# An attention block with its feed-forward and a second attention: VectorE's part of the softmax shift one round later, and sums pinned behind the last minimum of scores

## The chip, the cores and the metric

The kernel runs on one core of a Trainium2 chip. The core has a matrix engine (TensorE, PE in the profile; its weight loads are PEld), a vector engine (VectorE, DVE), an engine for activation functions (ScalarE, ACT), a general engine (GpSimd, POOL) and an engine that here only issues transfers (SyncE, SP). Each engine takes its instructions in the order in which they stand in its own queue and waits, at an instruction, for the semaphores that this one names; all that stands behind it on this engine waits too. The metric is the device time of one execution in microseconds (us), lower is better.

## The reference

The reference works on x of shape (2, 1024, 1024), all in float32:

```python
x = x + attn_a(layernorm(x))   # 32 heads of 32, rotary, causal, plus an adapter prefix of 10 tokens
x = x + ffn(layernorm(x))      # x @ W_base.T + b, plus 8 low-rank experts weighted by a sparsemax router
x = x + attn_b(layernorm(x))   # 8 heads of 16, not causal, softmax divided by sqrt(128)
x = x + ffn(layernorm(x))      # the same weights again
```

Only the attentions matter for the change. For each head they need softmax(q k^T * scale) v, with the row's maximum subtracted before the exponential.

## The kernel before, in words

**Stages.** Attention A with the projections of its queries, keys and values fills roughly the first 1320 us; then come its output projection, the first feed-forward, attention B and the second feed-forward, partly interleaved.

**Units and rounds.** Attention is cut into units. A unit of A is one batch element b, one group g of four heads (128 partitions) and one half n of the 1024 queries: 32 units, named A{b}_{g}_{n}. A unit of B is named in the same manner (8 units). Every unit passes over its scores twice. The first pass (`s_mm`, `s_post`) multiplies queries by keys into the PSUM tile `sc` (L308); VectorE writes the masked, scaled and negated scores to `pr` and keeps the running minimum in `part` or `nmax` (L321, one instruction for each score tile and head, with a short one that reads the accumulator); ScalarE takes the exponential and sums it into `sums` (L329). From `nmax` and the logarithm of `sums` the unit makes its shift (`shift`, L332 to L351): m = nmax + bias - ln(sums), split into three bfloat16 parts so that they add up to it. TensorE transposes the shift into rows (`shift_rows`, tile `st_A`; evacuated by L218 or L220). The second pass (`t_mm`) computes the scores transposed in the tile `st` with the shift added as a small matmul (L376 and L378), so that one exponential on ScalarE (L489) gives finished probabilities `pt`, which GpSimd masks on the diagonal (L385) and TensorE multiplies with the values (L400).

The loop of `attend` walks through rounds r. Each round has the scores of two heads of one step of the first pass and two heads of one step of the second. `sc` and `st` share a tag of two PSUM buffers and are drawn in turn, so the scores of round r+1 reuse the tile of the scores of round r, and TensorE's L308 waits there until VectorE's minima of round r are done. A unit with n=0 has fewer keys than one with n=1; after the last row of scores of a unit its shift is written in the same round.

**Fill.** Between rounds `Filler` lets TensorE work on the projections of later groups. These are Strassen-like: `seven` does seven block products instead of eight; its sums and combinations on VectorE are `factors` (sums of weight blocks, L594 and L597, tiles s, s_v, wqk, wv) and the lines L652 to L671, which combine PSUM results y and z with SBUF blocks. `rotate` (L792, L793 on VectorE; L796, L797 on GpSimd) applies the rotary embedding to queries and keys. Weights arrive by `v_load` (L682, a single buffer of 1 MB for two groups) and `qk_load` (L688, two buffers).

**The adapter.** `adapter_scores` multiplies queries by adapter keys into the tile `as`, and VectorE takes the maximum (L735), the difference (L737), the sum (L740) and the reciprocal (L741), with an exponential on ScalarE between (L738). `as`, the transposes of the shift and those of x for the second batch element share one PSUM bank.

**What sets the order.** The queues of TensorE and, in attention A, of GpSimd are written by hand, in program order. The queues of VectorE and ScalarE are ordered by a planner, which lists instructions by when it believes them to be ready. Two ways hold it to an order: `tc.keep_in_program_order(r)` puts r behind the instruction of its engine that was traced just before it, and `tc.add_manual_dep` puts one instruction behind a named one. Neither makes an instruction wait for the other to finish. Before, the sums and combinations used the first: each stands behind whatever VectorE instruction was traced before it, which at the end of a unit is the last of its shift.

## Time and profile before

| what | us |
|---|---|
| median of 3 runs | 2521.57 (2521.26 to 2530.68) |
| the profiled execution's own time | 2524.32 |
| its span, first to last instruction | 2522.6 |
| TensorE busy | 2444.0 |
| VectorE busy | 1334.8 |
| ScalarE busy | 1092.2 |
| GpSimd busy | 501.0 |
| TensorE busy between 100 and 1320 us (attention A) | 1179.0 of 1220 |
| VectorE's waits for the logarithm at L346, 29 times | 47.6 |
| VectorE's waits for the logarithm at L340 (attention B), 7 times | 14.2 |

The granted TensorE clock of the execution was 0.992 of full speed. In a row of the profile "L321 DVE ... out<-in" names the line of the kernel, the engine, what is written and what is read; a row of waits gives who waited for whom, the total, how often and the longest; in a row of the order of time come start, duration, instruction and, in brackets, the idle time of the engine before it with what ended it.

### The profile page before, as it was taken

To read this page: it belongs to the slowest core of one execution; us is meant where nothing else is said; L and a number is where in the kernel's file an instruction comes from. 1 tells how busy PE (TensorE), PEld (TensorE's weight loads), DVE (VectorE), ACT (ScalarE), POOL (GpSimd) and SP (SyncE) were. 2 spreads that over 40 slices of the span, in tenths; PEclk is the share of its full clock that TensorE was granted. 3 is DMA by queue.
4 is the path that set the end of the run, shared out by engine and by line. 5 is a ranking of instruction groups with operands and counts; after the bars stand their busy time and mean duration, and the time that the engine had idled before them with its cause. 6 is when DMAs were issued, how large, how long until landed. Compare 5 with 4: busy or idle time off the path is not lost.

```text
span 2522.6 us, 60430 instructions
## 1 busy us (share of the span) xinstructions
PE 2444.0 (97%) x25477; PEld 1107.0 (44%) x25477; DVE 1334.8 (53%) x4120; ACT 1092.2 (43%) x2085; POOL 501.0 (20%) x800
## 2 busy tenths in 40 slices
PE   7889999999999999999999999999999999999999
PEld 4424444455344444445433445575333553333344
DVE  7665665566655666565520013456555765654243
ACT  2346666565655666566642000012445535554200
POOL 1332322222323233222200002101000101111120
PEclk9999999999999999999999999999999999999999
DMA  6622323332423333333222551120000310212121
GB/s 211 205 89 77 97 84 92 94 90 90 138 85 107 90 98 89 94 89 111 86 72 75 172 185 51 58 92 35 34 34 35 127 43 26 93 43 84 43 101 42
DMA packets 142512, 224.34 MB, mean 89 GB/s; under 512 B 12832, under 2 KB 73376, under 8 KB 142240
## 3 DMA queue, kind: packets, MB, share of 16 engines
q1 hardware_dynamic: 142240, 220.48, 27.3%
q8 instruction: 199, 3.26, 0.5%
q14 instruction: 73, 0.60, 0.1%
HBM read 168.01 MB, written 52.43 MB: 87 GB/s over the span
## 4 chain that ended last, share of the span: by engine, by line
PE 84%; DVE 7%; ACT 5%; DMA 2%; issue 1%; POOL 1%; SPq 0%; DVEq 0%; ACTq 0%; POOLq 0%
PE fo_f L207 11%; PE st L378 9%; PE fo_f L209 8%; PE sc L308 7%; PE op L207 6%; PE y_A L400 5%; PE y L209 5%; PE z L209 3%; PE op L209 3%; PE st L376 3%; PE x L209 3%; ACT pr_A L329 2%; PE y_B L400 2%; PE bq L207 2%; PE y_v L209 2%; DVE pr_A L321 2%
## 5 line engine op out<-in xcount | busy, mean ns | idle before, releaser
L489 ACT ACTIVATE pt<-st 128x1024 f32<-128x1024 f32 (+1 forms) x418 | 426.3, 1020 | 663.6 <-PE st L378 497.7
L329 ACT ACTIVATE pr_A<-pr_A,nmax_A 128x896 f32<-128x896 f32 (+7 forms) x512 | 390.0, 765 | 68.4 <-DVE nmax_A L321 67.7
L308 PE MATMUL sc<-kT,qT 32*128 32x512 f32 (+3 forms) x1536 | 329.3, 525 | 18.5 <-DVE nmax_A L321 13.6
L321 DVE CUSTOM_DVE_ANT_0 pr_A<-sc,mask 128x512 f32<-128x512 f32 (+3 forms) x512 | 250.9, 536 | 180.5 <-PE sc L308 94.4
L378 PE MATMUL st<-qT,kT 32*128 32x512 f32 (+3 forms) x1536 | 310.1, 491 | 0.0
L207 PE MATMUL fo_f<-wb,xt_f 128*128 128x512 f32 x558 | 252.9, 596 | 0.4 <-ACT hwT_f L1135 0.4
L321 DVE CUSTOM_DVE_ANT_0 pr_A<-sc,mask,part_A 128x512 f32<-128x512 f32 (+1 forms) x256 | 156.3, 647 | 162.4 <-PE sc L308 114.8
L225 POOL TENSOR_TENSOR xf<-xf,b_base 128x256 f32<-128x256 f32 x128 | 89.3, 729 | 762.0 <-DVE xn_f L247 457.8
L209 PE MATMUL fo_f<-wb,xt_f 128*32 128x512 f32 x1864 | 223.1, 598 | 0.0
L385 POOL TENSOR_SCALAR_AFFINE_SELECT pt<-pt 128x256 f32<-128x256 f32 x256 | 100.3, 410 | 543.7 <-ACT pt L489 543.7
L329 ACT ACTIVATE pr_B<-pr_B,nmax_B 128x1024 f32<-128x1024 f32 x128 | 145.5, 1140 | 39.9 <-DVE nmax_B L321 39.8
L400 PE MATMUL y_A<-pt,v 128*32 128x512 f32 (+3 forms) x1536 | 160.0, 502 | 1.3 <-POOL pt L385 1.3
L207 PEld LDWEIGHTS fo_f<-wb,xt_f 128*128 128x128 f32 x558 | 103.5, 193 | 113.7 <-issue 113.1
L308 PE MATMUL sc<-kq,qk 32*128 32x512 f32 x512 | 145.1, 643 | 3.5 <-DVE nmax_B L321 3.2
L207 PE MATMUL op<-wp,yt 128*128 128x512 f32 x338 | 145.7, 592 | 0.0
L378 PE MATMUL st<-rows_B,kq 32*128 32x512 f32 x512 | 144.7, 641 | 0.2 <-ACT pt L489 0.2
L378 PEld LDWEIGHTS st<-qT,kT 32*128 32x128 f32 x1536 | 133.9, 186 | 16.7 <-issue 11.6
L239 ACT ACTIVATE lv_f<-ve_f 128x1 f32<-128x1 f32 x32 | 6.5, 203 | 309.1 <-DVE ve_f L237 309.1
L376 PE MATMUL st<-rows_A,ones 3*128 3x512 bf16 (+3 forms) x768 | 128.0, 330 | 10.8 <-DVE nmax_A L321 10.8
L321 DVE CUSTOM_DVE_ANT_0 pr_B<-sc,mask,part_B 128x512 f32<-128x512 f32 x128 | 91.1, 747 | 81.3 <-PE sc L308 81.2
L308 PEld LDWEIGHTS sc<-kT,qT 32*128 32x128 f32 x1536 | 113.9, 185 | 35.1 <-DVE nmax_A L321 17.3
L376 PEld LDWEIGHTS <-ones 3*128 3x128 bf16 x768 | 37.1, 91 | 197.2 <-issue 189.7
(274 smaller groups left out, 3707.2 us busy)
## 6 DMA issues: line engine op xcount, KB each, us to landing
tt<-td SPq DMA_DIRECT2D x252, 256.0 KB, 2.8
wqk<-in_w_attnT SPq DMA_DIRECT2D x32, 512.0 KB, 5.2
xf<-x SPq DMA_DIRECT2D x32, 512.0 KB, 3.3
xa<-in_x SPq DMA_DIRECT2D x16, 512.0 KB, 6.0
wv<-in_w_attnT SPq DMA_DIRECT2D x8, 1024.0 KB, 5.3
yd<-ys SPq DMA_DIRECT2D x32, 256.0 KB, 2.8
yt<-yd SPq DMA_DIRECT2D x128, 64.0 KB, 2.0
xp<-in_x SPq DMA_DIRECT2D x32, 256.0 KB, 3.0
```

The source lines that it names most:

```text
L207: return pe.matmul(out, lhsT=lhsT, rhs=rhs, start=start, stop=stop, skip_group_check=True)
L209: pe.matmul(out[i : i + 32], lhsT=lhsT[:, i : i + 32], rhs=rhs, start=start, stop=stop, skip_group_check=True)
L225: pool.tensor_add(dst[:, i : i + 2 * P], a[:, i : i + 2 * P], b[:, i : i + 2 * P])
L239: act.activation(lv, ve, AF.Ln)
L308: yield w * COL, lambda: pe.matmul(dst[:, o : o + w], lhsT=self.qt[rows, qc : qc + P], rhs=self.kt[rows, c0 : c0 + w], start=True, stop=True)
L321: dve.tensor_tensor_reduce(pr[:, c0 : c0 + w], sc[:, i, o : o + w], m, -self.scale, BIG if c0 == 0 else self.part[:, col], ALU.add, ALU.mi ...
L329: tc.keep_in_program_order(act.activation(pr[:, :nk], pr[:, :nk], AF.Exp, bias=self.nmax[:, col], scale=-1.0, accum_out=self.sums[:, col]))
L376: yield w * COL / 4, lambda: pe.matmul(dst[:, o : o + w], lhsT=ones[three, :], rhs=self.rows[three, off : off + w], start=True, stop=False)
L378: yield w * COL, lambda: pe.matmul(dst[:, o : o + w], lhsT=self.kt[rows, kb * P : (kb + 1) * P], rhs=rhs, start=self.extra, stop=True)
L385: pool.affine_select(out=dg, in_=dg, compare_op=ALU.is_ge, fill=0.0, base=0, pattern=[[0, 2], [1, P]], channel_multiplier=-1)
L400: pe.matmul(self.y[32 * h : 32 * h + 32, off : off + w], lhsT=self.value(h, kb), rhs=pt[h // 2][:, h % 2, o : o + w], start=self.opens, st ...
L489: act.activation(pt[:, :, low_:wide_], st[:, :, low_:wide_], AF.Exp, scale=ts[0][0].scale)
```

## The change

`shift` is cut in two. `logs` keeps the logarithm on ScalarE and is still called in the round of the unit's last scores. The rest, on VectorE, is called one round later, after that round's `s_post`. A helper `pin` puts an instruction behind the last traced minimum (L321) on VectorE; the first instruction of the shift, and all the sums and combinations of the projections that were kept in program order, now go through it.

```diff
+    minimum = [None]
+
+    def pin(r):
+        if minimum[0] is not None:
+            tc.add_manual_dep(
+                r.ins, minimum[0].name,
+                mybir.DependencyInfo(mybir.DependencyClass.NoSync, mybir.DependencyReason.DATA), reason="behind the minimum",
+            )
+        return r
...
-                dve.tensor_tensor_reduce(
+                minimum[0] = dve.tensor_tensor_reduce(
...
-                )
+                ).ins
...
+        def logs(self):
+            self.ln = self.wk.tile([P, 16], F32, tag="ln", name=f"ln_{self.nm}", bufs=2)
+            act.activation(self.ln, self.sums, AF.Ln)
+
         def shift(self):
 
-            wk, nm = self.wk, self.nm
-            ln = wk.tile([P, 16], F32, tag="ln", name=f"ln_{nm}", bufs=2)
-            act.activation(ln, self.sums, AF.Ln)
+            wk, nm, ln = self.wk, self.nm, self.ln
...
-            dve.scalar_tensor_tensor(m, self.nmax, self.bias, ln, ALU.add, ALU.subtract)
+            pin(dve.scalar_tensor_tensor(m, self.nmax, self.bias, ln, ALU.add, ALU.subtract))
...
+            due, logs = logs, []
             for u, piece in ss:
                 u.s_post(piece, sp, sc)
                 t, nk, c0, w, o = piece
                 if sp == 1 and t == u.s_rows[-1][0] and c0 + w == nk:
-                    u.shift()
+                    u.logs()
+                    logs.append(u)
+            for u in due:
+                u.shift()
...
         def pin_sub(*a):
-            tc.keep_in_program_order(dve.tensor_sub(*a))
+            pin(dve.tensor_sub(*a))
 
         def pin_add(*a):
-            tc.keep_in_program_order(dve.tensor_add(*a))
+            pin(dve.tensor_add(*a))
...
-            tc.keep_in_program_order(dve.tensor_add(c[12], c[22], y))
+            pin(dve.tensor_add(c[12], c[22], y))
```

The last replacement is made alike at the other combinations of `seven`: L657, L663, L667 and L671. The `extra` branch of `shift` (attention B, L340) is pinned in the same way.

More of the change, by code (lines that the diff above doesn't have):

```diff
@@ L339, in shift @@
                 self.sh = sh = wide[0]
-                dve.scalar_tensor_tensor(sh[:, :, :, self.width].rearrange("p t h -> p (t h)"), self.nmax, self.bias, ln,
-                                         ALU.add, ALU.subtract)
+                pin(dve.scalar_tensor_tensor(sh[:, :, :, self.width].rearrange("p t h -> p (t h)"), self.nmax, self.bias, ln,
+                                             ALU.add, ALU.subtract))
                 return
@@ L450, in attend @@
         pts, queue = {}, deque()
+        logs = []
         for r in range(2 * len(t_steps) + 3):
@@ L656, in seven @@
             yield from product(7, y)
-            tc.keep_in_program_order(dve.tensor_add(c[21], c[12], y))
+            pin(dve.tensor_add(c[21], c[12], y))
             pin_sub(f[3], f[3], f[6])
@@ L662, in seven @@
             yield from product(5, z, stop=False)
-            tc.keep_in_program_order(dve.tensor_add(c[22], c[21], z))
+            pin(dve.tensor_add(c[22], c[21], z))
             settled(22)
@@ L666, in seven @@
             yield from product(4, y)
-            tc.keep_in_program_order(dve.tensor_sub(c[21], c[21], y))
+            pin(dve.tensor_sub(c[21], c[21], y))
             settled(21)
@@ L670, in seven @@
             yield from product(3, z, start=False)
-            tc.keep_in_program_order(dve.tensor_add(c[12], c[12], z))
+            pin(dve.tensor_add(c[12], c[12], z))
             settled(12)
```

## The prediction

> **What bounds the kernel now.** I read the page first: busy shares, then the chain that ended last.

> ```profile
> PE 2444.0 (97%) x25477; PEld 1107.0 (44%) x25477; DVE 1334.8 (53%) x4120; ACT 1092.2 (43%) x2085; POOL 501.0 (20%) x800
> PE 84%; DVE 7%; ACT 5%; DMA 2%; issue 1%; POOL 1%; SPq 0%; DVEq 0%; ACTq 0%; POOLq 0%
> ```

> TensorE is busy 2444.0 of 2522.6 us and is 84% of the chain; VectorE is on it only 7%. A change that touches no matmul can at most close TensorE's 78.6 us of idle time. The busy time by stretch puts most of that in attention A: 1220 - 1179.0 = 41 us of it lie between 100 and 1320 us. So I asked for TensorE's waits in 100 to 1300 us (engine, tile, line, what it waited for: total us, times, longest):

> ```profile
> PE sc L308 <- DVE nmax_A L321: 11.7, 10, 3.6
> PE st L376 <- DVE nmax_A L321: 10.8, 11, 2.4
> PE sc L308 <- POOL qT L797: 4.8, 4, 1.9
> PE st_A L209 <- DVE ae L737: 3.6, 10, 1.3
> PE z L209 <- DVE qT L663: 0.9, 1, 0.9
> PE z_v L209 <- DVE qT L667: 0.5, 1, 0.5
> ```

> Five of these end in VectorE, and the POOL one is fed by VectorE's rotation (L792). Their sum, 32 us, is about what the change can reach. What makes VectorE late is seen in its order of time at a unit's end (start, duration, instruction, idle time before it), with TensorE's line below:

> ```profile
> 993.34 0.08 DVE L321 DVE_READ_ACCUMULATOR2_ANT nmax_A<- 128x1 f32 x1
> 996.42 0.17 DVE L346 SCALAR_TENSOR_TENSOR m_A<-nmax_A,ln_A 128x16 f32<-128x16 f32 x1 [3.00 <-ACT ln_A L336]
> 997.54 0.32 DVE L351 TENSOR_TENSOR shift<-m_A,shift 128x16 bf16<-128x16 f32 x1
> 997.74 0.28 DVE L321 CUSTOM_DVE_ANT_0 pr_A<-sc,mask 128x128 f32<-128x128 f32 x1
> 999.11 0.07 DVE L321 DVE_READ_ACCUMULATOR2_ANT nmax_A<- 128x1 f32 x1
> 999.24 0.38 PE L308 MATMUL sc<-kT,qT 32*128 32x128 f32 x2 [1.11 <-DVE nmax_A L321]
> ```

> VectorE's last minimum ends at 993.4; then it stands for 3.00 us before L346, because the logarithm is queued on ScalarE behind the last exponentials. The next round's scores had been written by 995.9, but their four minima (1.45 us, 997.74 to 999.19) are queued behind the shift, and TensorE's next sc, which reuses the same PSUM tile, waits 1.11 us for them.

> **The change, part by part.** It adds no arithmetic, matmul or DMA. In the built program the sequences of TensorE, ScalarE, GpSimd and SyncE are the same as before; only VectorE's order differs. The six shift instructions of a unit (L346 to L351; L340 in attention B) now stand behind the next round's minima, and some sums (L594, L597, L652 to L671) stand elsewhere between the same two groups of minima.

> (a) Shift behind the minima, ends of n=1 units. At 999.24: minima need the scores (995.88) and a free VectorE, so 995.9 + 1.45 = 997.4; TensorE asks at 998.14 (end of L376). The 1.11 us goes. At 456.85 the wait is 3.65: the last minimum ends at 447.17, L346 waits to 449.64, the shift runs to 450.99, and a block of rotation and sums (450.86 to 455.34, 4.48 us) then precedes the minima. Now that block starts at 447.2: 447.2 + 4.5 + 1.45 = 453.1, and TensorE asks at 453.2. At 611.75 (2.02): scores at 607.5, minima done 608.95, asked at 609.74. The other seven (0.87, 0.27, 0.23, 0.27, 1.98, 1.11, 0.22) have the same form. All ten: 11.7 us. Behind the minima the six instructions (1.36 us at 996.42, the logarithm being done by then) stand before the following round's minima, which had 0.64 us of idle there and 1.1 us more because the scores now end earlier by that wait: hidden. If that cover were gone it would cost 0.7 us at an end. Their reader, TensorE's transposes of the shift, comes more than 20 us later.

> (b) n=0 ends. L735 and L737, which empty the PSUM bank that the shift's transposes reuse, were queued behind L346:

> ```profile
> 945.28 0.18 DVE L346 SCALAR_TENSOR_TENSOR m_A<-nmax_A,ln_A 128x16 f32<-128x16 f32 x1 [0.95 <-ACT ln_A L336]
> 945.93 0.32 DVE L737 TENSOR_TENSOR ae<-as,am 128x160 f32<-128x160 f32 x1
> 946.31 0.41 PE L209 MATMUL st_A<-identb,shift 128*32 128x128 bf16 x16 [0.26 <-DVE ae L737]
> ```

> Without it: 945.2 (the as matmuls end) + 0.32 + 0.03 + 0.32 = 945.9, and TensorE is free at 946.04. Nine sites of 0.26 and 0.2 of the 1.28 at 178.5: 2.6 us.

> (c) st L376 <- L321, 10.8 us. These minima are queued behind k's rotation and the next weights' sums. The total work ahead is unchanged. At three sites (0.35, 0.50, 0.94) L597, 1.2 us, now stands ahead of an L671 that waits for TensorE, and fills that wait: all 1.8. At five sites the sums are laced between dependent steps. There each dependent step leaves 0.03 to 0.11 idle and independent neighbours overlap by 0.08 (starts against ends in the rows above), so 0.4 each: 2.0. At 237.38 one L594 of 0.68 moves into idle time: 0.6. Sum 4.4; bounds 0 and 10.8.

> (d) Ends where a combination was pinned behind L351. L663 at 145.57 becomes possible at 142.1: the z wait of 0.86 goes, the rotation starts some 2.5 us sooner, and the two waits on POOL (1.93 and 1.44 at 153 and 155) shrink; TensorE passes there 2.5 us earlier in all. At 763.93 two sums (1.21 + 1.10) now precede L667, still 1.35 us sooner: 1.35. Sum 3.85. The first end, at 99.06, gives 0.4.

> (e) Losses. At 632 to 637 us L671, L597 and the first L594 now stand ahead of L735:

> ```profile
> 629.40 0.38 SPq L682 DMA_DIRECT2D wv<-in_w_attnT  x1
> 633.31 0.32 DVE L735 TENSOR_REDUCE am<-as 128x16 f32<-128x160 f32 x1
> 635.52 0.69 DVE L597 TENSOR_TENSOR s_v<-wv 128x512 f32<-128x512 f32 x1
> 634.57 0.66 PE L213 MATMUL xt_a<-ident,xn 128*128 128x128 f32 x4
> ```

> L597 reads weights issued at 629.40; such a load lands after 5.3 us (median in the DMA view), so 634.6. Then L597 0.69, L594 0.69, L735 0.32, L594 0.68, L737 0.32, less overlaps: 637.0. Queued behind it on TensorE is xt_a at 634.57, which reuses the bank that L737 reads: 2.5 us lost. The weights of the other value projections are issued tens of us before their sums. Three ends (538.6, 694.1, 929.0) put one 0.67 to 1.2 us operation ahead of L735: 0.4 + 0.6 + 0.4. One in project_b near 2020: below 0.3, against a similar gain beside it; taken as nothing. Sum 3.9. In attention B L340 lies under fill matmuls, and no wait of TensorE follows it: nothing gained or lost.

> [...] L348 to L351 took 0.67 to 0.80 each at 607.3 to 610.4, against 0.18 to 0.32 at 996, while GpSimd ran L796 and L797. [...] I take the row and keep 2 for the range.

> **Sum.** 11.7 + 2.6 + 4.4 + 3.85 + 0.4 = 22.95; minus 3.9 = 19.0 off the profiled execution's span of 2522.6 (its own time 2524.3, 1.7 around the span): 2505.3. That execution lies 2.75 above the median shown, so 2521.6 - 19.0 = 2502.6; I say 2503.

> **Rivals.**
> 1. The waits re-form (chance 0.14). TensorE arrives earlier, VectorE's block ahead of it is as long, so (a) keeps half (5.9), (c) and (d) give 2, (b) 2.6, minus 3.9: 7 us, 2515. For it: VectorE's work is conserved. Against: VectorE idles 47 us in L346 alone, and at 999, 611 and 456 its freed time exceeds the wait.
> 2. The change does nothing (0.05): TensorE is 97% busy and fill hides it; 2521. Against: the waits above are TensorE's own idle time.
> [...]

> **How the numbers follow.** My forecast has 0.75. Half a percent, 12.6 us, is about what this kernel's measurement can tell from no change: faster is below 2509. The forecast's own range is 2496 (half of (c)'s rest, 3.2, and losses halved, 2, and rounding) to 2511 (no gain from (c), the lock's 2, (d) halved). Of the forecast 0.71 lies below 2509, plus 0.03 of rival 1: faster 0.77. Same: 0.04 + 0.11 + 0.05 less a little = 0.18. Slower 0.05. With rival 1 the range for 8 in 10 is 2495 to 2515.

> **What would show it.** Right: L346's idle row (47.6 us over 29) is nearly gone; sc L308 <- nmax_A falls from 11.7 to under 2; st_A <- ae from 3.6 to about 1 plus the new losses; TensorE's idle time from 78.6 to about 60; a new wait xt_a L213 <- ae L737 of about 2.5 near 630. Wrong: an equal wait of sc or st on L321 one round later, or L348 to L351 with means of 0.7.

## The result, and the profile after

The changed kernel takes 2491.64 us (median; 2486.35 to 2496.83) against 2521.73 before: a ratio of 0.9874, 95% interval 0.9856 to 0.9892, 30.1 us. The forecast was 2503, with a range from 2495: the direction held, the gain was taken too small by 11 us. The profiled execution after took 2490.82 us (span 2489.1), the one before 2524.32 (span 2522.6); between these two the gain is 33.5 us.

Busy shares and the chain that ended last, on the page of the kernel after (to be held against the first fence of the prediction):

```profile
PE 2433.3 (98%) x25477; PEld 1101.6 (44%) x25477; DVE 1339.2 (54%) x4120; ACT 1090.0 (44%) x2085; POOL 499.1 (20%) x800
PE 88%; DVE 6%; issue 2%; DMA 2%; ACT 1%; POOL 1%; SPq 0%; DVEq 0%; ACTq 0%; POOLq 0%
```

TensorE's idle time fell from 78.6 to 2489.1 - 2433.3 = 55.8 us, 22.8 less. But its busy time fell too, by 10.7 us, with the same 25477 matmuls. The forecast's sum has no term for that. TensorE's waits between 100 and 1300 us after the change (total us, times, longest; these lines lie 11 to 18 lower in the file now, so L308, L321, L346, L376, L735 and L737 are now L319, L332, L359, L389, L753 and L755):

```profile
PE st_A L209 <- DVE ae L755: 5.7, 7, 2.6
PE st L389 <- DVE nmax_A L332: 4.1, 6, 1.8
PE xt_a L213 <- issue: 2.5, 1, 2.5
PE akp L209 <- DVE ae L755: 2.2, 1, 2.2
PE sc L319 <- DVE nmax_A L332: 2.0, 1, 2.0
...
PE sc L319 <- POOL qT L815: 0.6, 1, 0.6
```

The scores' wait for the minima went from 11.7 us to one wait of 2.0, `st`'s from 10.8 to 4.1, GpSimd's from 4.8 to 0.6. `st_A`'s wait for `ae` rose from 3.6 to 5.7. VectorE's 47.6 us ahead of L346 are down to 2.4. The unit's end that the prediction shows at 993 to 999 us reads, after, on VectorE and then on TensorE:

```profile
976.42 0.08 DVE L332 DVE_READ_ACCUMULATOR2_ANT nmax_A<- 128x1 f32 x1
976.42 0.17 DVE L359 SCALAR_TENSOR_TENSOR m_A<-nmax_A,ln_A 128x16 f32<-128x16 f32 x1
976.50 0.68 DVE L670 TENSOR_TENSOR v<-v,y_v 128x512 f32<-128x512 f32 x1
977.10 0.17 DVE L360 TENSOR_SCALAR m_A<-m_A 128x16 f32<-128x16 f32 x1
...
978.00 0.23 DVE L364 TENSOR_TENSOR shift<-m_A,shift 128x16 bf16<-128x16 f32 x1
978.10 0.28 DVE L332 CUSTOM_DVE_ANT_0 pr_A<-sc,mask 128x128 f32<-128x128 f32 x1
```

```profile
976.64 0.38 PE L319 MATMUL sc<-kT,qT 32*128 32x128 f32 x2
```

The four minima end at 976.42; only then does the shift run, without waiting for its logarithm, and the next `sc` starts at 976.64 with no idle time in front.

### The profile page after: what moved, and what is told of

It is laid out like the page before. It is cut to its first block, busy times and chain, and to the rows that moved or that the text cites. A ratio compares the mean times of both kernels' runs of the same rounds, so it can differ in the third digit from the quotient of the medians.

```text
span 2489.1 us, 60414 instructions
## 1 busy us (share of the span) xinstructions
PE 2433.3 (98%) x25477; PEld 1101.6 (44%) x25477; DVE 1339.2 (54%) x4120; ACT 1090.0 (44%) x2085; POOL 499.1 (20%) x800
## 4 chain that ended last, share of the span: by engine, by line
PE 88%; DVE 6%; issue 2%; DMA 2%; ACT 1%; POOL 1%; SPq 0%; DVEq 0%; ACTq 0%; POOLq 0%
PE fo_f L207 11%; PE st L391 9%; PE fo_f L209 7%; PE sc L319 7%; PE op L207 6%; PE y_A L413 5%; PE y L209 5%; PE z L209 3%; PE st L389 3%; PE op L209 3%; PE y_v L209 3%; PE x L209 3%; PE y_B L413 2%; PE bq L207 2%; DVE pr_A L332 2%
## 5 line engine op out<-in xcount | busy, mean ns | idle before, releaser
L340 ACT ACTIVATE pr_A<-pr_A,nmax_A 128x896 f32<-128x896 f32 (+7 forms) x512 | 389.9, 765 | 47.2 <-DVE nmax_A L332 46.5
L332 DVE CUSTOM_DVE_ANT_0 pr_A<-sc,mask 128x512 f32<-128x512 f32 (+3 forms) x512 | 251.1, 537 | 200.0 <-PE st L391 103.5
L319 PE MATMUL sc<-kT,qT 32*128 32x512 f32 (+3 forms) x1536 | 329.1, 525 | 4.4 <-DVE nmax_A L332 3.6
L332 DVE CUSTOM_DVE_ANT_0 pr_A<-sc,mask,part_A 128x512 f32<-128x512 f32 (+1 forms) x256 | 156.2, 647 | 147.3 <-PE sc L319 98.7
L209 PE MATMUL fo_f<-wb,xt_f 128*32 128x512 f32 x1864 | 223.6, 599 | 0.0
L340 ACT ACTIVATE pr_B<-pr_B,nmax_B 128x1024 f32<-128x1024 f32 x128 | 145.6, 1140 | 41.2 <-DVE nmax_B L332 41.2
L319 PE MATMUL sc<-kq,qk 32*128 32x512 f32 x512 | 144.3, 640 | 3.7 <-DVE nmax_B L332 3.3
L332 DVE CUSTOM_DVE_ANT_0 pr_B<-sc,mask,part_B 128x512 f32<-128x512 f32 x128 | 91.2, 747 | 79.8 <-PE sc L319 79.7
L389 PE MATMUL st<-rows_A,ones 3*128 3x512 bf16 (+3 forms) x768 | 127.8, 329 | 4.1 <-DVE nmax_A L332 4.1
L332 DVE CUSTOM_DVE_ANT_0 pr_B<-sc,mask 128x512 f32<-128x512 f32 x128 | 83.4, 687 | 75.9 <-PE sc L319 75.9
L319 PEld LDWEIGHTS sc<-kT,qT 32*128 32x128 f32 x1536 | 113.5, 184 | 18.6 <-issue 9.2
```

The source lines that it names most:

```text
L209: pe.matmul(out[i : i + 32], lhsT=lhsT[:, i : i + 32], rhs=rhs, start=start, stop=stop, skip_group_check=True)
L319: yield w * COL, lambda: pe.matmul(dst[:, o : o + w], lhsT=self.qt[rows, qc : qc + P], rhs=self.kt[rows, c0 : c0 + w], start=True, stop=True)
L332: minimum[0] = dve.tensor_tensor_reduce(pr[:, c0 : c0 + w], sc[:, i, o : o + w], m, -self.scale, BIG if c0 == 0 else self.part[:, col], AL ...
L340: tc.keep_in_program_order(act.activation(pr[:, :nk], pr[:, :nk], AF.Exp, bias=self.nmax[:, col], scale=-1.0, accum_out=self.sums[:, col]))
L389: yield w * COL / 4, lambda: pe.matmul(dst[:, o : o + w], lhsT=ones[three, :], rhs=self.rows[three, off : off + w], start=True, stop=False)
```

## What a wait of TensorE costs

Three numbers from the trace split each span: idle time; time lost to the clock (the trace records the steps in which TensorE was granted half its clock; a step of 3.4 us loses 1.7); and the rest.

| profiled execution | span | idle | lost to the clock | rest |
|---|---|---|---|---|
| before | 2522.6 | 78.6 | 21.1 | 2422.9 |
| after | 2489.1 | 55.8 | 15.7 | 2417.6 |
| difference | 33.5 | 22.8 | 5.4 | 5.3 |

The rest is lost overlap. A group of matmuls mostly starts 0.07 us or more before the modelled end of the one ahead of it (median 0.27 us between 100 and 1300 us), and an idle row counts only from that end. So a wait costs its row and this overlap. Take the same 40 matmuls around a wait in both executions: at 946.31 (`st_A`) a wait shown as 0.26 was worth 0.33, at 999.24 (`sc`) one shown as 1.11 was worth 1.39. At the other waits that went whole the surplus is 0.07 to 0.08 us for `st_A` and `st`, 0.21 to 0.28 for `sc` and 0.62 for `y_A`. Stretches of 200 matmuls of attention A in which neither execution has a wait or a step take the same time to 0.01 us, save two (near 300 and 1060) that are 0.5 and 0.3 us longer before with no row to show it.

The clock is seen at the unit's end where `sc` waited 3.65 us at 456.85. Busy time by stretch, before and then after, from about the same matmul on (columns: stretch, length, then busy us and instructions of PE, PEld, DVE, ACT and POOL, granted clock, DMA share, GB/s):

```profile
456.00:466.00 10.00, 9.15 (x170) 6.29 (x174) 5.79 (x20) 5.38 (x19) 2.81 (x5) 0.66 0.11 31
```

```profile
444.00:454.00 10.00, 9.35 (x262) 6.81 (x256) 6.80 (x24) 5.84 (x17) 2.82 (x7) 1.00 0.40 110
```

0.66 over 10 us is one step of 6.8 us at half clock. TensorE looks 92% busy there, but its 170 matmuls take 9.17 us from the first start to the next group's, and the same 170 take 7.05 us after the change, with a wait of 0.65 us among them (the 262 of the second row are partly others). The wait and its step went together, and so did the steps at the wait of 2.02 us (611.75) and behind three of 0.47, 0.72 and 0.67 us (764 to 770). In exchange four waits of the changed kernel bring or lengthen one: 2.05 at 102, 2.23 at 156, 2.53 at 618 and 2.65 at 682.

## Experiments

Theory A: the forecast's list of waits was about right, and it priced each wait too low, because lost overlap and halved clock come on top of the idle time. Theory B: a wait costs its idle time (and a little lost overlap, the refill of the expectations), and the surplus comes from terms sized wrongly, the sums above all. "Profiled" is the profiled execution.

**The shift alone**, with sums and combinations as before:

```diff
         def pin_sub(*a):
-            pin(dve.tensor_sub(*a))
+            tc.keep_in_program_order(dve.tensor_sub(*a))
...
-            pin(dve.tensor_add(c[12], c[22], y))
+            tc.keep_in_program_order(dve.tensor_add(c[12], c[22], y))
```

> The shift alone is written a round later and pinned behind the minima; sums and combinations keep the order that they have in the kernel before. Theory A (a wait of TensorE costs more than its idle time: 0.07 to 0.35 us to refill behind each, and 1.7 us of halved clock behind one of about 2 us or more): terms (a) and (b) of the forecast, 14 us of idle time, plus some 20 waits x 0.25 = 5, plus two or three halved steps = 4: about 23 us, 2499 us. The wait of xt_a near 620 us and the large one of st_A near 682 us are not there, since the sums that caused them stay behind the adapter's ae. Theory B (a wait costs its idle time, and the surplus of the result comes from the sums): 14 us, about 2507.

Measured: 2493.62 us (ratio 0.9899, 0.9883 to 0.9916; before is 2520.38 here), 26.8 us. In attention A, taken between the same two matmuls (90 and 1320 us of before), the stretch is 26.2 us shorter: idle 15.7, clock 5.1, rest 5.4. That is nearer to A's sum (14 + 4 + 5) than to B's 14. The wait of `xt_a` near 620 is absent, as expected; the one of `st_A` near 682 is not: 1.46 us of it stay (at 679.49), and waits of 1.07 us on `ae` are new at 450.79 and 757.99. At 679 the moved chain, laced with VectorE's part of the rotation, stands ahead of the minima and `ae` without any sum; at the other two the chain and two sums or combinations behind it do.

**The pins alone**, with the shift in its own round, unpinned:

```diff
                     u.logs()
-                    logs.append(u)
-            for u in due:
-                u.shift()
+                    u.shift()
...
-            pin(dve.scalar_tensor_tensor(m, self.nmax, self.bias, ln, ALU.add, ALU.subtract))
+            dve.scalar_tensor_tensor(m, self.nmax, self.bias, ln, ALU.add, ALU.subtract)
```

> Only the sums and combinations are pinned behind the last minimum; the shift stays in its own round, unpinned. Theory A: terms (c) and (d) less (e), 4.4 us of idle time, but the two waits of 2.5 us that (e) makes each halve the clock once: 4.4 + 1 - 3.4 = 2 us, about 2520 us. Theory B: the sums carry the surplus, so 4.4 + 11 = 15 us, about 2506.

Measured: 2506.19 us (0.995, 0.9934 to 0.9966), 14.2 us, on B's number. But not for B's reason: in attention A idle time fell by 10.8 us where I had expected 4.4, and the stretch by 12.4. The terms of the sums were indeed too small (6.7 us of `st`'s waits went, not 4.4; and freed of L351 the combinations let the minima at 456 start 2.2 us sooner against TensorE). Of the two halved steps that A expected one came (behind the wait of 2.90 us near 630); the other wait stayed at 0.60. In all, the loss to the clock in attention A is that of before, 12.0 us. So this run speaks for the mis-sized terms of B and against A's number; the price of a wait it doesn't settle. The two halves give 26.8 + 14.2 = 41 us alone and 30.1 together: about 8 us of idle time (chiefly at 146, 153, part of 456, 703, 765, 1076) go with either.

**Few long waits against many short ones.** Reductions that nobody reads are put on VectorE ahead of the minima, seven at 7 places or four at 21:

```diff
+    def hold(n):
+        for _ in range(n):
+            minimum[0] = pin(dve.tensor_reduce(idle, mask[:, :HF], AX.X, ALU.max)).ins
+        held[0] = n
...
+            if ss and not ss[0][0].extra and r in range(190, 271, 12):
+                hold(7)
             for u, piece in ss:
                 u.s_post(piece, sp, sc)
```

The other kernel has `range(190, 271, 4)` and `hold(4)`; in both the first minimum that follows is pinned behind the reductions.

> The price of a long wait by itself. The kernel after, with seven reductions that nobody reads put on VectorE ahead of the minima of scores at seven places in the second half of attention A (output unchanged). Seven reductions of 512 elements are about 4.5 us; VectorE has 1 to 2 us to spare in such a round, so TensorE should wait some 2.5 to 3.5 us at each place, about 20 us in all. Theory A (a wait of about 2 us or more also halves the clock for a 3.4 us step, 1.7 us, and costs up to 0.35 us of refill): the span grows by about 1.7 times the added idle time, 35 us, with a step of halved clock at most of the seven places. Theory B (a wait costs its idle time and the refill): 1.1 to 1.2 times, about 23 us, and no more halved steps than in the kernel after.

> The price of short waits. The kernel after, with four such reductions (about 2.5 us) at 21 places in the same stretch, so that TensorE should wait 0.5 to 1.3 us at each, 10 to 20 us in all. Theory A: short waits don't halve the clock, so the span grows by 1.2 to 1.3 times the added idle time (the refill alone), and the steps of halved clock are those of the kernel after. Theory B: the same, 1.1 to 1.2 times. The two runs together: A expects a clearly higher price for one us of idle time in the run with few long waits, B the same price in both.

Measured: 2506.25 us and 2506.17 us, 14.6 and 14.5 us above the kernel after. Between the same two matmuls (900 and 1250.5 us of after), profiled:

| | longer by | idle | clock | rest | per us of idle |
|---|---|---|---|---|---|
| few long | 17.5 | 10.6 | 6.8 | 0.1 | 1.65 |
| many short | 16.0 | 12.9 | 1.7 | 1.4 | 1.25 |

The waits did not come out as planned: the seven places gave two waits of 4.22 us and a few below 1 us, and of the 21 places two gave 2.38 us and the others 1.74 or less. The prices are A's (1.7, and 1.2 to 1.3). Each wait of 4.22 halved the clock for 6.8 us; those up to 1.74 cost no step. The first wait of 4.22, and the stretch around it with a granted clock of 0.66 (columns as above):

```profile
972.79 1.22 PE L326 MATMUL sc<-kT,qT 32*128 32x512 f32 x2 [4.22 <-DVE nmax_A L339]
```

```profile
970.00:980.00 10.00, 7.21 (x94) 3.59 (x94) 4.74 (x11) 6.34 (x11) 0.41 (x1) 0.66 0.11 35
```

The two of 2.38 us differ in this; the second kernel, the row with the wait and those behind it, first without a step, then with one:

```profile
970.42 1.06 PE L209 MATMUL y_v<-s_v,tt 128*32 128x128 f32 x32
973.86 0.39 PE L400 MATMUL st<-rows_A,ones 3*128 3x512 bf16 x2 [2.38 <-DVE nmax_A L339]
973.86 0.70 PE L326 MATMUL sc<-kT,qT 32*128 32x512 f32 x2
974.07 0.61 PE L402 MATMUL st<-qT,kT 32*128 32x512 f32 x2
```

```profile
1126.29 0.61 PE L400 MATMUL st<-rows_A,ones 3*128 3x512 bf16 x2 [2.38 <-DVE nmax_A L339]
1126.30 1.22 PE L326 MATMUL sc<-kT,qT 32*128 32x512 f32 x2
1126.67 1.08 PE L402 MATMUL st<-qT,kT 32*128 32x512 f32 x2
```

The same matmuls take 0.70 and 0.61 us behind the first wait, 1.22 and 1.08 behind the second. In attention A, over all profiled executions here, a wait below 1.7 us that stood alone never had a step, one from 1.8 to 2.4 us had one in some executions, and those from 2.5 to 4.22 us had one with a single exception (2.79 near 106 us). Short waits close together had one at three places: two of 1.25 and 1.32 us within 2 us (151 to 153, the pins alone), the three of 0.47, 0.72 and 0.67 us within 5 us (764 to 770, before), and two of 0.46 and 0.84 us (105 and 108, the second execution of the anchor). Outside attention A a single wait of 0.81 us had one too (1838, the first execution of the anchor); why is open.

In the traces all steps of an execution begin and end on one grid of 3.413 us: before, those at 456.36 and 613.37 us lie 46.00 steps apart, those at 456.36 and 1937.74 us 434.00. From one execution to the next the grid lies elsewhere against the kernel: the first step begins 46.76 us after the span's start before and 47.94 after, so 2.39 and 0.15 us past a multiple of 3.413. That a wait falls differently against the grid might be why the same 2.38 us count once and not the other time (argued, not tested). A length from which a wait brings a step is not shown: waits of 1.8 to 2.65 us, shorter than one step, had one at some places and at others not.

**The adapter's `ae` as an anchor.** The kernel after, with sums pinned behind `ae` where that is later than the last minimum:

```diff
-            dve.tensor_add(e3, s3, nmx[:, :, None].to_broadcast([P, 16, NA]))
+            minimum[0] = dve.tensor_add(e3, s3, nmx[:, :, None].to_broadcast([P, 16, NA])).ins
```

> The kernel after, with the adapter's ae taken as the instruction behind which later sums are pinned, so that no sum written after it stands ahead of it. Theory A: the wait of xt_a (2.53 us, near 618) goes whole with its halved step and refill, 4.2; of the one of st_A near 682 (2.65) the 1.26 of the sum goes, and as what is left is below 2 us its halved step too, 3; three waits of 0.4 to 0.65 give 1.5: 8.7 us below the kernel after, about 2483 us. Theory B (idle time only): 2.5 + 1.3 + 1.5 = 5.3, about 2486.5.

Measured: 2483.73 us (0.9857, 0.9842 to 0.9871), 7.9 below the kernel after; A had 8.7, B 5.3 (8.2 where the two were measured side by side, below). In attention A it is 7.8 us shorter: idle 4.5, clock 3.4. Two of the three short waits went (0.41 each); the one of 0.65 at 448 stayed. Its wait of `st_A`, and VectorE near 613, where the kernel after has L615 ahead of L753:

```profile
PE st_A L209 <- DVE ae L755: 3.6, 5, 1.5
```

```profile
613.34 0.33 DVE L753 TENSOR_REDUCE am<-as 128x16 f32<-128x160 f32 x1 [0.90 <-PE as L209]
613.70 0.32 DVE L755 TENSOR_TENSOR ae<-as,am 128x160 f32<-128x160 f32 x1
...
615.06 0.69 DVE L615 TENSOR_TENSOR s_v<-wv 128x512 f32<-128x512 f32 x1 [0.22 <-DMA wv<-in_w_attnT]
```

**The shift two rounds later:**

```diff
-            due, logs = logs, []
+            due, older, logs = older, logs, []
```

> The kernel after, with the shift written two rounds later than the logarithm, not one. It tests whether small VectorE instructions take 0.6 to 0.8 us for running beside GpSimd's 0.7 us instructions. If so, the chain that took 3.62 us beside GpSimd's subtractions at 96.5 us takes 1.4 to 1.8 in its new place, where those have ended, and TensorE's wait of 2.05 us for the scores' minima at 102 us goes; the chain that stood at 674.7 now stands near 680, where four GpSimd subtractions run from 678.6 to 681.8, and stays slow (over 3 us), with the wait of st_A of 2.65 us as large or larger. Net about -3.5 at the first, 0 to +2 at the second: 2488 to 2492 us. If the length of the chain is not GpSimd's doing, it is 3 us or more at both places, and the waits stay.

Measured: 2495.01 us (0.9903, 0.9888 to 0.9918), 3 above what I expected at most. The lengths came as expected: beyond GpSimd's subtractions the small instructions take 0.16 to 0.23 us each, and at 685 us, beside them, the chain takes 3.87 with three other instructions laced in. The wait of `sc` near 102 fell from 2.05 to 0.32. That of `st_A` near 682, which I had expected to stay or grow, fell from 2.65 to 1.54. But the freed time did not reach TensorE: the next user of the queue, the adapter's transposed weights `awTA`, is still copied at 104.2, and TensorE waits 2.79 us for it. At some unit starts, where the chain is now laced with `ae`, waits of `st_A` of 0.6 to 0.7 us appear in place of none to 0.41, and `atA`, a transpose of the adapter's weights, waits 1.16 us at 641.

**GpSimd's subtractions moved to VectorE**, a direct test of the length of the moved chain:

```diff
-                fill.chore(("T1", b), lambda t1=t1, b11=b11: in_pieces(pool.tensor_sub)(t1, t1, b11))
+                fill.chore(("T1", b), lambda t1=t1, b11=b11: pin_sub(t1, t1, b11))
```

> The kernel after, with the subtractions of xnT that GpSimd runs at 95.9 to 101.4 and again at 678.6 to 681.8 us done on VectorE, later. If the shift's five small instructions took 0.63 to 0.68 us each at 96.5 because GpSimd ran beside them, they take 0.16 to 0.25 us there now, the chain about 1.4 us in place of 3.62, and the minima of scores end 2 us sooner, so that TensorE's wait of 2.05 us at 102 goes or falls below 0.5; the chain at 674.7, which runs beside GpSimd's rotation, stays near 4 us. If GpSimd is not the cause, the chain at 96.5 keeps its 3.6 us. VectorE gets 5.6 us of added work, 2.8 at each of the two places, so the time itself is not the test: within 3 us of the kernel after.

Measured: 2491.17 us in one execution. VectorE's chain and TensorE's next scores in the kernel after, with GpSimd's row, and then without the subtractions:

```profile
95.89 5.50 POOL L608 TENSOR_TENSOR xnT<-xnT,xnT 128x256 f32<-128x256 f32 x8
```

```profile
96.70 0.63 DVE L360 TENSOR_SCALAR m_A<-m_A 128x16 f32<-128x16 f32 x1
97.37 0.68 DVE L361 CAST shift<-m_A 128x16 bf16<-128x16 f32 x1
...
99.44 0.67 DVE L364 TENSOR_TENSOR shift<-m_A,shift 128x16 bf16<-128x16 f32 x1
```

```profile
102.09 1.65 PE L319 MATMUL sc<-kT,qT 32*128 32x512 f32 x4 [2.05 <-DVE nmax_A L332]
```

```profile
96.76 0.17 DVE L360 TENSOR_SCALAR m_A<-m_A 128x16 f32<-128x16 f32 x1
96.97 0.20 DVE L361 CAST shift<-m_A 128x16 bf16<-128x16 f32 x1
...
97.66 0.23 DVE L364 TENSOR_TENSOR shift<-m_A,shift 128x16 bf16<-128x16 f32 x1
```

```profile
100.42 1.13 PE L319 MATMUL sc<-kT,qT 32*128 32x512 f32 x4 [0.32 <-DVE nmax_A L332]
```

3.62 us became 1.33 and the wait of 2.05 became 0.32. Beside GpSimd each of these instructions on 16 elements per partition, from the second of the chain on, takes 0.63 to 0.68 us, about as long as one of GpSimd's (5.50 / 8 = 0.69). The chain at 674, still beside GpSimd's rotation, took 5.0 us: three of its instructions 0.71 to 0.79 us each, and four of VectorE's own larger ones between them. In this kernel the time saved is spent again: `y` waits 3.15 us in place of 1.96 at 113, `st_A` 3.49 in place of 2.65 at 682, and `awTA` is waited for at 103 (0.84 us).

**Versions that may beat both.** Side by side on one chip: the kernel after; the anchor; the anchor with the shift two rounds later and written behind `late(r, begun)`, so behind `ae`; and a mixed one that does the latter for attention A except its first unit.

```diff
-            for u in due:
-                u.shift()
...
             spent = late(r, begun)
+            for u in due:
+                u.shift()
```

> A version that may beat the kernel after: the adapter's ae as the instruction behind which later sums are pinned, and the shift written two rounds after the logarithm and behind that ae, so that neither the sums nor the shift chain stand ahead of it. Theory A: all that the first gives (2484 us) and, near 694 us of the kernel before, the 1.47 us wait of st_A shrinks by the shift chain's share (under 0.5 left): 2482 us. If the chain, now behind ae, delays the copy of st_A to SBUF (rows) or the following minima, it is as long as or longer than the kernel with the anchor alone: 2484 to 2488.

> The kernel after again, beside the three versions below on one chip, so that they are compared with it and not only with the kernel before: 2491 to 2493 us, with about 56 us of idle time of TensorE in the profiled execution and 15 to 19 us lost to halved clock.

> The kernel with the adapter's ae as an instruction behind which sums are pinned, again: 8 us below the kernel after (2483 to 2485), as idle time is 3.6 us lower and the two halved steps at its waits of 2.53 and 2.65 us (3.4 us) are absent.

> The kernel with that and the shift two rounds later behind ae, again. Its profiled execution had 54.3 us of idle time against 52.2 with the anchor alone, so the two should not differ by more than 3 us: 2482 to 2487.

> As the one before, but the first unit and attention B keep the shift one round later, since there two rounds cost idle time (near 105 us a wait of 2.77 in place of one of 2.05; in attention B about 2 us). Idle time should be that of the anchor alone less the waits of st_A near 448, 598 and 682 us (0.63 + 0.25 + 1.47), about 49.5 us, and the time 2 to 3 us below the anchor's: 2480 to 2483. If moving the shift behind ae only moves waits elsewhere, it is equal to the anchor's.

| kernel | median us | ratio to before, interval | idle |
|---|---|---|---|
| after | 2491.61 | 0.9884, 0.9871 to 0.9898 | 57.2 |
| anchor | 2483.40 | 0.9849, 0.9835 to 0.9862 | 51.5 |
| anchor, two rounds | 2485.83 | 0.9867, 0.9854 to 0.9881 | 52.4 |
| mixed | 2482.88 | 0.9851, 0.9838 to 0.9864 | 50.1 |

The first measurement of the third was 2482.32. The anchor is 8.2 us better than the kernel after, with intervals that don't meet. Moving the shift further gives nothing on top, and the 2 to 3 us expected of the mixed one did not come (0.5, well inside the intervals): the waits of `st_A` at 448, 598 and 682 us of the kernel after do go, as expected, but one of 1.16 us near 634 (transposes of the adapter's weights) and one of 0.7 near 690 (`y_A` on GpSimd's mask) take their place. The best is the kernel after with one more line.

## Why the prediction was wrong, step by step

What failed is the step under the first fence, "A change that touches no matmul can at most close TensorE's 78.6 us of idle time", and with it the sum: 19.0 us of idle time taken as 19.0 us of time, with lost overlap and the halved clock put at nothing. (As a bound 78.6 us was never reached; as a price, one us of time for one of idle time, it was wrong.) In attention A (between the same two matmuls) the stretch became 27.35 us shorter: idle 20.4, clock 1.7, rest 5.2. The five terms themselves came to 19.0, the very net of the forecast, but by errors of both signs, which is luck:

| term | forecast | idle time that went |
|---|---|---|
| (a) shift behind the minima, ten n=1 ends | 11.7 | 11.7: all ten waits are 0 |
| (b) `ae` no longer behind L346 | 2.6 | 2.5 |
| (c) `st` on the minima | 4.4 (0 to 10.8) | 6.7 |
| (d) combinations, and the first end | 4.25 | 5.2 |
| (e) losses | -3.9 | -7.1 |
| in no term: `y_A` on GpSimd's mask, 702.80 | 0 | 1.3 |

- (a) and (b): right, and the shift alone removes every wait of (a). The cover of the moved chain held at every end but two.
- (c): the pins alone bring it, the shift alone none. At 843 and 1070 1.46 and 1.14 us went, where I had counted no more than 0.4 at a laced end. The term was mis-sized, inside its bounds.
- (d): it became 3.3 near 150, with 0.4 lost there at the adapter's keys, and 1.8 near 765. The shift alone frees nearly all of the first: what held the scores there was the shift more than the combination. The first end came to 0.2, not 0.4: its wait of 2.05 us at 102 is new, and waits of 1.16 and 0.63 us behind it went.
- (e): the wait of `xt_a` came as forecast, 2.53 us at 618, and by the cause named. After, VectorE, SyncE's load and TensorE:

```profile
610.38 0.38 SPq L700 DMA_DIRECT2D wv<-in_w_attnT  x1
```

```profile
615.55 0.69 DVE L615 TENSOR_TENSOR s_v<-wv 128x512 f32<-128x512 f32 x1 [1.91 <-DMA wv<-in_w_attnT]
...
617.72 0.32 DVE L755 TENSOR_TENSOR ae<-as,am 128x160 f32<-128x160 f32 x1
```

```profile
618.14 1.08 PE L213 MATMUL xt_a<-ident,xn 128*128 128x128 f32 x4 [2.53 <-issue]
```

So did 0.41 at 523 and at 909, as forecast. Two were missed: 0.65 at 448, and 2.65 at 682 (694 before) where I had 0.6. There the moved chain runs beside GpSimd's rotation:

```profile
677.23 0.67 DVE L363 CAST shift<-m_A 128x16 bf16<-128x16 f32 x1
677.93 0.81 DVE L364 TENSOR_TENSOR shift<-m_A,shift 128x16 bf16<-128x16 f32 x1
...
679.99 1.26 DVE L615 TENSOR_TENSOR s<-wqk 128x512 f32<-128x512 f32 x1
...
681.52 0.32 DVE L755 TENSOR_TENSOR ae<-as,am 128x160 f32<-128x160 f32 x1
```

```profile
677.11 0.73 POOL L814 TENSOR_TENSOR qr<-qr,sin 128x256 f32<-128x256 f32 x1
677.92 0.73 POOL L815 TENSOR_TENSOR qT<-qT,qr 128x256 f32<-128x256 f32 x1
```

The chain takes 4.05 us, 1.4 of them VectorE's part of the rotation laced in. The minima start at 678.62, though their scores were written at 676.91, and L615 (1.26 us) stands between them and `ae`. Without L615, with the anchor, 1.47 of the 2.65 us stay: that is the chain's part. The 2 us that the forecast keeps for the range and calls the lock's are shown by no run. What the traces show in their place is the length of VectorE's small instructions beside GpSimd. Before, three or more of a chain took 0.6 us and more at one end of 32 (0.67 to 0.80 at 607); after, at two (0.63 to 0.68 near 97, 0.67 to 0.81 near 677), where TensorE then waited 2.05 and 2.65 us. At the ends near 145, 450, 605 and 763 of before, where GpSimd's work overlaps the moved chain by 1.3 to 1.8 us, at most one instruction of it took 0.6 us or more, and the waits are 0.65 us at most, but for one on `ae` at 156 (2.23; 1.83 before).
- In no term: of the waits before, the prediction's list left out this one among others, and it went whole:

```profile
PE y_A L400 <- POOL pt L385: 1.3, 1, 1.3
```

It goes with the wait of `st_A` some 8 us ahead of it in the queue, which the change made longer: where that is 1.46 us or more it is below 0.1 (the shift alone, the anchor, the shift two rounds later), where that is 0.60 or nothing (the pins alone; the anchor with two rounds) 0.69 and 0.70 are left. So about half of it is paid for by that longer wait; what removed the other half is open.
- Attention B, "nothing gained or lost": there and in the feed-forwards 2.5 us of idle time and 1.7 of clock went. The wait of 1.73 us of `xt_b` near 2020 goes with the shift alone and stays with the pins alone.
- Lost overlap was in no term: 5.2 us in A, over thirty-odd waits that went (0.07 us at one of `st` or `st_A`, some 0.28 at one of `sc`).
- The clock was in no term either: 5.4 us in the pair of profiles. Of these 1.7 belong to a wait near 47 us that the change doesn't touch: this step was 6.8 us long in one execution and 3.4 in the other, and again 6.8 in a further execution of the kernel after. Repeats of one kernel differ by up to 10 us along with the clock (from 2486.35 at a mean of 0.996 to 2496.83 at 0.992), so the share of the clock in the medians is known only roughly: the gain between the medians is 30.1, not 33.5. The mean granted clock is 0.9933 over the 24 executions of the kernel before that stand beside the runs, and 0.9940 over ten of the kernel after; an estimate from these is 17 and 15 us lost, so some 2 us of gain.
- The sum of the miss: of the 11 us between the forecast gain of 19.0 and the 30.1 measured, some 4 are idle time in no term (1.3 of `y_A`, 2.5 behind attention A), 5 lost overlap and, by that estimate, 2 the clock.

Rival 1 was wrong as a whole, for all that it had its place: new waits did form. Nor was the kernel slower: the chain beside GpSimd did delay minima, but at two ends of 31.

## What to carry to other kernels

Where TensorE bounds a kernel, price a wait by more than its idle row: add the overlap that it breaks (0.07 to 0.28 us at most waits here), and the chance of a clock step of 1.7 us, which in attention A came behind waits of 2.5 to 4.22 us with one exception, behind some of 1.8 to 2.4 us, and at three places behind two or three short ones within some 5 us. Short waits that stand well apart were cheaper here than one long wait of the same sum (1.25 against 1.65 us for one us of idle time). When work is moved behind one instruction (here the minima), list what else on that queue TensorE waits for (here `ae`) and pin behind the later of the two. A chain of tiny VectorE instructions had two prices here, 0.2 us each alone and 0.6 to 0.8 beside GpSimd's rotation or subtractions (0.7 us each), so look at GpSimd's row at the place that it is moved to.
